# Length-1 LSTM of the first superchunk as one set of seven products, layer 2 weight products in their own tile, four pieces at other places

## The chip, the core and the metric

The kernel runs on one core of one Trainium2 chip. The metric is the device time of that core in microseconds (us). The kernel before takes 1908.22 us, the median of three runs (1907.53 to 1908.26). The profiled execution has a span of 1905.4 us, and places in the trace are given as us from its start.

TensorE is called PE in the profile (PEld its weight loads), VectorE DVE, ScalarE ACT, GpSimd POOL and SyncE SP. "L1110" is line 1110 of the kernel.

## The reference

The input x is [128 batches, 64 steps, 256 channels] in float32, with a 64 x 64 adjacency matrix. Four layers each add a residual, x = x + layer(relu(layernorm(x))):

```python
# layer 0: two products with batch normalizations, after one aggregation by the normalized adjacency
# layer 1: two graph convolutions, then LSTMs over windows of p = 1, 2, 3, 4 steps
h = relu(einsum('ts,bsh->bth', adj, x @ Wg0 + bg0))
h = relu(einsum('ts,bsh->bth', adj, h @ Wg1 + bg1))
for p in range(1, 5):
    nw = T // p
    wins = h[:, :nw * p, :].reshape(B * nw, p, H)          # windows without overlap
    last = lstm_last(Wih[p - 1], Whh[p - 1], bih[p - 1], bhh[p - 1], wins)   # zero initial state
    h = h.at[:, arange(nw) * p + (p - 1), :].set(last)     # the last step of each window
# layer 2: causal attention over the 64 steps, with Wqkv and Wo
# layer 3: attention with 4 heads, masked by the adjacency, with W
```

With p = 1 the initial state is zero, so a window is one step: three gates (input, candidate, output) from one product with Wih, then h = sigmoid(o) * tanh(sigmoid(i) * tanh(g)).

## The kernel before

The 8192 tokens are in 16 chunks of 512 tokens (8 batches by 64 steps), and the middle layers take them in 8 superchunks of two chunks. First layer 0 is computed for all chunks, because its batch normalizations need statistics of everything. Then, for superchunk 0, the two graph convolutions of layer 1 are computed alone ("first_convolutions", chunks 0 and 1); after them comes the long part of the LSTMs, superchunk after superchunk; layers 2 and 3 follow.

Products of channels by channels are computed by 2 x 2 blocks with seven products in place of eight. The seven right operands are three blocks b11, b21, b22 of the hidden state and four differences t1 = b12 - b11, t3 = b22 - b12, t2 = b22 - t1, t4 = b21 - t2 (`differences`, L313 to L316). The block rows are the two halves of the channels; the columns are two halves of the tokens. The weights' sums, which the left operands need, are formed once.

**The length-1 LSTM** is `single` (L1275): seven products by three gates, each a matmul at L1307, kinds 2, 1, 5, 6, 3, 7, 4 in that order. ScalarE copies products from PSUM (L1327), VectorE adds others to them (L1331), ScalarE applies sigmoid and tanh (L1312, L1320), GpSimd or VectorE multiplies the gates (L1317), and VectorE writes the new state into hT (L1323). The differences are all formed on GpSimd. In superchunks 1 to 7 the token halves are the first and the last 32 steps of all 16 batches, 512 columns each. In superchunk 0 there are two sets, one for each chunk, with halves of 256 columns, so that the first can begin while chunk 1's convolutions are still under way.

**The longer LSTMs** are `lstm` with p = 2, 3, 4. Each begins with a product g (L1123) for the first step, whose gates ScalarE reads from PSUM at L1110; that frees the banks in which the next products, y, z and x at L1152, are summed. Differences of the new state (hd, L313 on VectorE) precede the products with it. Gate sums are VectorE's at L1161, gate functions ScalarE's at L1066.

**The order around them is written out by hand.** `lstms` is a generator: its yields are numbered as units, 0 to 3 in the length-1 LSTM, 4 to 7 in length 2, 8 to 13 in length 3, 14 to 21 in length 4. At each unit, pieces of other work are issued: the convolutions of the next superchunks, the residual of the superchunk before, and `ahead`, which prepares layer 2. Tables say at which unit each piece comes: CONV and BEGUN (in superchunk 0 FIRST and BEGUN_FIRST) for the convolutions, RESIDUAL, AHEAD, LATE, and FINAL for the last superchunk. All engines take their instructions in that order; a piece that waits holds what was issued to its engine after it.

- A convolution's pieces are: load (normalization L898 and transposes L986 on VectorE, to DRAM and back, and the load of x), the sum L284, layer norm statistics, its application in two halves (factor nmr, L194, on VectorE, then two L196 on ScalarE for each half), aggregate, copies, product v, bound, product u, bias (L933), aggregate, and twice `to_hT` (L938, ScalarE).
- The pieces of `ahead` are: put, reorder, statistics, first half of the application (L194 and two L196), second half, and squares with put.

**Weight products.** Layer 2 uses Wq Wk^T and Wv Wo, formed once during layer 0 in `weight_products` (L717): matmuls L730, copies L732 into wqkv_sb, the tile from which Wqkv was read, and a store to DRAM at L733 (products_far, wqv_far in the profile). Two tiles ("ws", two buffers) in the same pool take the weights whose sums are formed for the LSTMs. Later the pool is closed, and the tile "early", the input of chunks 0 and 1, lies over the same memory. Pools wait by tile: a new tile waits for every user of the tiles whose memory it takes.

The lines that decide where pieces come:

```python
for n, _ in enumerate(lstms(sc, hTs[sc])):
    for u in todo.pop(n, ()):
        next(u)
```

Of the kernel before, what the change touches and what calls it, by code (L numbers as in the profile page):

```python
# [8 lines left out]
F32 = mybir.dt.float32  # L9
# [4 lines left out]
P = 128  # L14
# [5 lines left out]
def kernel(  # L20
# [22 lines left out]
    nc = tc.nc  # L43
    B, T, D = x.shape
    H0 = w1t.shape[1]
    KD = D // P
# [6 lines left out]
    CH = 512  # L53
    NJ = CH // P
    NB = CH // T
    NCH = B * T // CH
    SUP = 2
# [251 lines left out]
    def differences(engine, dst, b11, b12, b21, b22, third=None):  # L309


        t1, t2, t3, t4 = dst
        return [lambda: engine.tensor_tensor(t1, b12, b11, OP.subtract),  # L313
                lambda: ((third or engine).tensor_tensor(t3, b22, b12, OP.subtract),
                         engine.tensor_tensor(t2, b22, t1, OP.subtract)),
                lambda: engine.tensor_tensor(t4, b21, t2, OP.subtract)]  # L316
# [80 lines left out]
    class Seven1:  # L397
# [28 lines left out]
        def part(self, m, j):  # L426
            return z1whole[self.c][m][:, :, halves2[j]]
# [161 lines left out]
    with tc.manual_schedule(engines={mybir.EngineType.PE, mybir.EngineType.DVE,  # L589
# [27 lines left out]
        for c in range(2, NCH - 1):  # L617
            a, z = sevens[c], sevens.get(c - 1)
# [3 lines left out]
            b = sevens[c + 1] = Seven1(c + 1) if c + 1 < NCH - 1 else None  # L622
# [36 lines left out]
        c = NCH - 1  # L659
# [27 lines left out]
    with tc.manual_schedule(engines={mybir.EngineType.PE}):  # L687
        banks = product2([0, 1], True)
        close_l0()


        stage, close_stage = pool("stage", 1)
        wqkv_sb = stage.tile([P, KD, 3 * D], F32, name="wqkv_sb")
        wo_sb = stage.tile([P, KD, D], F32, name="wo_sb")
        bg0_sb = stage.tile([P, D], F32, name="bg0_sb")
        bg1_sb = const.tile([P, D], F32, name="bg1_sb")
        wg1_st = stage.tile([P, KD, D], F32, name="wg1_st")
        nc.sync.dma_start(wqkv_sb, wqkv.rearrange("(k p) f -> p k f", p=P))
        nc.sync.dma_start(wo_sb, wo.rearrange("(k p) f -> p k f", p=P))
        nc.sync.dma_start(bg0_sb, bg0.partition_broadcast(P))  # L700
        nc.sync.dma_start(bg1_sb, bg1.partition_broadcast(P))
        nc.sync.dma_start(wg1_st, wg1.rearrange("(k p) f -> p k f", p=P))

        wt = stage.tile([P, 3 * KD, D], F32, name="wt")
        c1 = stage.tile([P, KD, P], F32, name="c1")

        def weight_transposes(blocks):
            for f in blocks:
                ps = bank(f"wt_{f}")
                for k in range(KD):  # L710
                    nc.tensor.transpose(ps[:, k * P : (k + 1) * P],
                                        wqkv_sb[:, k, f * P : (f + 1) * P], ident)
                nc.vector.tensor_copy(wt[:, f, :], ps[:, :D])

        products = [wqkv_sb[:, :, i * D : (i + 1) * D] for i in range(2)]
        products_far = dram.tile([P, KD, 2 * D], F32, tag="wqv", name="wqv_far", bufs=1)

        def weight_products():
            for m in range(KD):
                ps = bank(f"c1_{m}")  # L720
                nc.tensor.matmul(ps[:, :P], bg0_sb[:, m * P : (m + 1) * P], adjt_bd, start=True,
                                 stop=True)
                nc.scalar.copy(c1[:, m, :], ps[:, :P])
                nc.scalar.mul(nc1[:, m, :], ps[:, :P], -1.0)
            for a in range(KD):
                for dst, lhs, rhs in ((products[0], 0, wt[:, KD : 2 * KD, :]),
                                      (products[1], 2 * KD, wo_sb)):
                    ps = bank(f"wp_{a}_{lhs}")
                    for f in range(KD):
                        nc.tensor.matmul(ps[:, :D], wt[:, lhs + f, a * P : (a + 1) * P],  # L730
                                         rhs[:, f, :], start=(f == 0), stop=(f == KD - 1))
                    nc.scalar.copy(dst[:, a, :], ps[:, :D])  # L732
            nc.scalar.dma_start(products_far, wqkv_sb[:, :, : 2 * D])  # L733
            ps = bank("c2")
            for k in range(KD):
                nc.tensor.matmul(ps[:, :D], c1[:, k, :], wg1_st[:, k, :], start=(k == 0),
                                 stop=(k == KD - 1))
            return ps

        def weight_sums(p, q):
            w = stage.tile([P, 16, P], F32, tag="ws", name=f"ws_{p}_{q}", bufs=2)
            for i, src in enumerate((wih_t, whh_t)):
                nc.sync.dma_start(
                    w[:, 8 * i : 8 * i + 4, :].rearrange("p (k c) f -> p k (c f)", k=KD),
                    src[p - 1].rearrange("(k p) f -> p k f", p=P)[:, :, q * D : (q + 1) * D])
            yield
            v = w.rearrange("p (i b) f -> p i b f", i=2)
            for dst, a, b, op in ((4, 1, 3, OP.add), (5, 4, 0, OP.subtract), (6, 0, 1, OP.subtract),  # L750
                                  (7, 2, 5, OP.subtract)):
                nc.gpsimd.tensor_tensor(v[:, :, dst], v[:, :, a], v[:, :, b], op)
            far = dram.tile([P, 15, P], F32, tag=f"ws{p}{q}", name=f"wfar_{p}_{q}", bufs=1)
            nc.sync.dma_start(far[:, :9], w[:, :9])
            nc.sync.dma_start(far[:, 9:], w[:, 10:])
            wfar[p, q] = far
            yield

        wanted = [(p, q) for p in range(2, SKIP + 1) for q in GATES]
# [3 lines left out]
    with tc.manual_schedule(engines={mybir.EngineType.PE, mybir.EngineType.DVE,  # L763
# [3 lines left out]
        for c in range(2, NCH - 1):  # L767
            a, b, z = sevens[c], sevens.get(c + 1), sevens.get(c - 1)
# [64 lines left out]
    with tc.manual_schedule(engines={mybir.EngineType.PE}):  # L833
        c = NCH - 1
# [438 lines left out]

    KINDS1 = {1: 0, 2: 1, 4: 2, 5: 3, 6: 4, 7: 5, 3: 6}

    def single(b, m, name, yields):

        wide = b[0, 0].shape[1:]  # L1280
        gates = l1.tile([P, 4, KD, CH], F32, tag="gates", name=f"gates_{name}", bufs=1)
        cells = l1.tile([P, KD, CH], F32, tag="cell", name=f"cell_{name}", bufs=1)
# [3 lines left out]
        def folded(a):  # L1286
            return a.rearrange("p (a b) -> p a b", b=wide[1]) if len(wide) > 1 else a
# [2 lines left out]
            return (more if j else cells)[:, c, :m] if g == 2 else gates[:, 2 * g + j, c, :m]  # L1290

        t = []
        for i in range(4 * m // (2 * CH)):
            part = l1.tile([P, 7 * (T // 3) * NB], F32, tag="xd", name=f"xd_{name}_{i}", bufs=2)
            t += [folded(part[:, a : a + m]) for a in range(0, 2 * CH, m)]
        for f in differences(nc.gpsimd, t, b[0, 0], b[0, 1], b[1, 0], b[1, 1]):
            f()
        right = {1: b[0, 0], 2: b[1, 0], 3: b[1, 1], 4: t[3], 5: t[0], 6: t[1], 7: t[2]}
        ys, xs_ = [[bank(f"{n}_{name}_{g}", tag) for g, tag in enumerate(tags)]
                   for n, tags in (("y1", "yyz"), ("x1", "zxx"))]  # L1300
# [4 lines left out]
        def product(kind):  # L1305
            for g in range(3):
                nc.tensor.matmul(folded(ps(g, kind)), wih1[:, g, KINDS1[kind], :], right[kind],  # L1307
                                 start=kind in (2, 5, 1), stop=True, skip_group_check=True)
# [16 lines left out]
        def copy(dst, kind):  # L1325
            for g in range(3):
                nc.scalar.copy(at(g, *dst), ps(g, kind))  # L1327

        def add(dst, kind):
            for g in range(3):  # L1330
                nc.vector.tensor_add(at(g, *dst), at(g, *dst), ps(g, kind))  # L1331

        product(2)
        copy((0, 0), 2)
        product(1)
        add((0, 0), 1)
        for g in range(3):
            act(g, 0, 0)
        cell(nc.gpsimd, 0, 0)
        if 0 in yields:  # L1340
            yield
        product(5)
        copy((1, 1), 5)
# [1 line left out]
        product(6)  # L1345
        copy((0, 1), 6)
        state(0, 0)
        if 1 in yields:
            yield
        product(3)  # L1350
        add((0, 1), 3)
        for g in range(3):
# [7 lines left out]
        act(2, 1, 1)  # L1360
        state(0, 1)
        cell(nc.vector, 1, 1)
        if 2 in yields:
            yield
        product(4)
        act(0, 1, 0, ps(0, 4))
        tanh(1, 1)
# [3 lines left out]
        tanh(1, 0)  # L1371
        state(1, 1)
        state(1, 0)
        if 3 in yields:
            yield

    def lstms(sc, hT):
        hv = hT.rearrange("p k (t b) -> p k t b", t=T)

        def views(part):  # L1380
            return {(k, j): part(hv[:, k, j * T // 2 : (j + 1) * T // 2, :]) for k in range(KD)
                    for j in range(2)}

        if sc:
            yield from single(views(lambda a: a.rearrange("p t b -> p (t b)")), CH, f"{sc}_1", range(4))
        else:
            for i in range(SUP):
                yield from single(views(lambda a: a[:, :, i * NB : (i + 1) * NB]), CH // 2, f"{sc}_1_{i}",
                                  (1, 3))
        for p in range(2, SKIP + 1):  # L1390
            yield from lstm(p, hv, f"{sc}_{p}", p == SKIP and sc < NCH // SUP - 1)

# [52 lines left out]
    RESIDUAL = (0, 3, 4), (2, 5, 6)  # L1445
    CONV = (3, 4, 4, 5, 6, 7, 8, 9, 10, 10), (3, 4, 4, 11, 12, 13, 14, 15, 16, 17, 18, 20)
    BEGUN = (11, 13, 14, 16), (17, 19)
    BEGUN_FIRST = (13, 15, 16, 18), (19, 21)
    FIRST = (0, 2, 3, 4, 4, 5, 6, 7, 8, 9, 10, 11, 12, 12), (3, 6, 7, 8, 8, 13, 14, 15, 16, 17, 18, 19, 20, 20)
    AHEAD = (4, 5, 7, 8, 14, 15), (6, 7)  # L1450
    LATE = 5, 6, 8, 9
    IDLE = {5: 4, 7: 18, 9: 10, 13: 14, 15: 8}
    FINAL = (4, 5, 10, 12, 12, 14), (6, 7, 11, 14, 14, 16)
# [595 lines left out]
```

## Time and profile before

| | us | share of the span |
|---|---|---|
| PE busy | 1869.7 | 98% |
| DVE busy | 1238.2 | 65% |
| ACT busy | 1017.2 | 53% |
| POOL busy | 578.4 | 30% |
| g of length 2 to 4, L1123 | 184.1 | |
| y, z, x of length 2 to 4, L1152, by operands: x<-xd | 285.6 | |
| span | 1905.4 | |

A page of the profile gives each engine's busy time, the granted TensorE clock, the chain of work that ended last, and the groups of instructions with, after the bar, their busy time, the mean of one in ns, and the idle time ahead of them with what ended it ("2.1 <-DVE gates L1161 1.7": 2.1 us idle, of which 1.7 were ended by that instruction). A line of the chain of waits gives start, length and what. A line of a timeline gives start, length, engine, line, operation, tiles and count, and in brackets the idle time before it and its releaser. A line of the table by windows gives the stretch, its length, busy time and count of PE, PEld, DVE, ACT and POOL, the granted clock (1.00 is full), the busy share of the DMA engines, and GB/s.

Matmuls of 512 columns follow each other every 0.86 us, those of 256 columns every 0.43 us. PE is busy nearly everywhere, so what matters are the places where it is not, and which instruction ends each wait there.

### The profile page before, as it was taken

The numbers are of one execution on the slowest core, as the hardware profiler recorded it, in microseconds if no ns is written. First come the engines' busy times: TensorE is split into PE (matmuls) and PEld (weight loads), VectorE is DVE, ScalarE is ACT, GpSimd is POOL, SyncE is SP. The second block draws the span as 40 slices with busy tenths as digits, with TensorE's granted clock in tenths as the row PEclk, the third lists the DMA queues.
The fourth block names the chain that finished last, engine by engine and source line by source line (L and its number), as shares of the span: only waits on it lengthen the run. The fifth ranks groups of instructions, "written<-read, shape, count | busy, mean of one in ns | idle before, by whom it ended". The sixth has DMA issues, their size and how long they took to land.

```text
span 1905.4 us, 39237 instructions
## 1 busy us (share of the span) xinstructions
PE 1869.7 (98%) x15119; PEld 1489.5 (78%) x15119; DVE 1238.2 (65%) x3157; ACT 1017.2 (53%) x2309; POOL 578.4 (30%) x766
## 2 busy tenths in 40 slices
PE   8999989999999999999999999999999999999998
PEld 6877866886897789689689679868959967777776
DVE  6768745567566666667657666665565567776776
ACT  5766535446456455555645644655565544444453
POOL 5856622123222222322322232222122113332332
PEclk9999989999999999999999999999999999999999
DMA  3223642134333533333433443333144245454433
GB/s 113 79 67 148 223 175 93 58 117 172 117 128 128 160 128 112 104 119 138 150 116 129 149 138 133 133 111 109 52 146 141 101 139 150 136 154 143 135 112 112
DMA packets 111403, 241.48 MB, mean 127 GB/s; under 512 B 11504, under 2 KB 74864, under 8 KB 111216
## 3 DMA queue, kind: packets, MB, share of 16 engines
q1 hardware_dynamic: 110192, 237.09, 37.0%
q8 instruction: 120, 1.97, 0.4%
q0 software_dynamic: 320, 1.05, 0.2%
q10 hardware_dynamic: 704, 0.82, 0.1%
q14 instruction: 67, 0.55, 0.1%
HBM read 170.50 MB, written 68.42 MB: 125 GB/s over the span
## 4 chain that ended last, share of the span: by engine, by line
PE 82%; DVE 8%; ACT 4%; POOL 2%; issue 2%; DMA 1%; SPq 0%; DVEq 0%; ACTq 0%
PE x L1152 22%; PE z L1152 11%; PE g L1123 7%; PE y L1152 5%; PE v L1539 5%; PE x L1307 3%; PE p_q L1546 3%; PE y L1307 3%; PE X L1735 3%; PE v L913 3%; PE X L423 2%; PE X L499 2%; PE u L927 2%; PE Y L1735 1%; PE Y L423 1%
## 5 line engine op out<-in xcount | busy, mean ns | idle before, releaser
L1161 DVE TENSOR_TENSOR gates<-gates,x 128x128 f32<-128x128 f32 (+2 forms) x384 | 118.3, 320 | 314.2 <-PE x L1152 312.0
L1152 PE MATMUL x<-xd,wset 128*128 128x128 f32 (+2 forms) x1280 | 285.6, 311 | 2.1 <-DVE gates L1161 1.7
L1152 PE MATMUL x<-hd,wset 128*128 128x128 f32 (+2 forms) x1152 | 246.7, 303 | 0.0
L1210 POOL TENSOR_TENSOR gates<-gates 128x512 f32<-128x512 f32 (+2 forms) x48 | 74.9, 1560 | 521.8 <-ACT gates L1066 521.8
L1152 PEld LDWEIGHTS x<-xd,wset 128*128 128x128 f32 x1280 | 202.1, 190 | 20.1 <-DVE gates L1161 6.1
L1066 ACT ACTIVATE gates<-gates,bias 128x256 f32<-128x256 f32 (+4 forms) x384 | 170.4, 490 | 65.0 <-DVE gates L1161 61.6
L1152 PEld LDWEIGHTS x<-hd,wset 128*128 128x128 f32 x1152 | 185.1, 191 | 5.0
L1123 PE MATMUL g<-hT,wset 128*128 128x256 f32 (+2 forms) x576 | 184.1, 474 | 1.9 <-DVE hT L1077 1.1
L1123 PEld LDWEIGHTS g<-hT,wset 128*128 128x128 f32 x576 | 108.4, 190 | 70.8 <-issue 38.0
L1158 ACT COPY gates<-y 128x128 f32<-128x128 f32 (+2 forms) x192 | 54.2, 293 | 194.4 <-PE y L1152 193.8
L1152 PE MATMUL z<-hs,wset 128*128 128x128 f32 (+2 forms) x768 | 154.0, 303 | 0.0
L1152 PEld LDWEIGHTS z<-hs,wset 128*128 128x128 f32 x768 | 119.8, 191 | 3.3
L1158 ACT COPY gates<-x 128x128 f32<-128x128 f32 (+2 forms) x192 | 56.5, 295 | 93.8 <-PE x L1152 92.9
L1161 DVE TENSOR_TENSOR gates<-gates,z 128x128 f32<-128x128 f32 (+2 forms) x384 | 104.5, 315 | 0.1
L1066 ACT ACTIVATE gates<-x,bias 128x128 f32<-128x128 f32 (+2 forms) x192 | 74.7, 389 | 49.1 <-PE x L1152 46.2
L1152 PE MATMUL z<-hT,wset 128*128 128x128 f32 (+1 forms) x512 | 97.1, 302 | 0.0
L1152 PE MATMUL x<-hs,wset 128*128 128x128 f32 (+2 forms) x384 | 84.9, 303 | 0.0
L1152 PE MATMUL y<-xd,wset 128*128 128x128 f32 (+2 forms) x384 | 78.2, 306 | 3.9 <-ACT gates L1110 3.9
L1152 PE MATMUL y<-hd,wset 128*128 128x128 f32 (+2 forms) x384 | 80.1, 311 | 1.9 <-DVE hd L313 1.9
L1221 ACT ACTIVATE gates<-cell 128x256 f32<-128x256 f32 (+2 forms) x144 | 55.3, 384 | 49.9 <-DVE cell L1220 49.8
L1110 ACT ACTIVATE gates<-g,bias 128x512 f32<-128x512 f32 (+2 forms) x144 | 72.3, 557 | 17.7 <-PE g L1123 17.6
L1554 POOL TENSOR_TENSOR s<-s,mx 128x256 f32<-128x256 f32 (+2 forms) x33 | 40.4, 1225 | 129.6 <-DVE mx L1553 121.8
(328 smaller groups left out, 4278.9 us busy)
## 6 DMA issues: line engine op xcount, KB each, us to landing
wset<-wfar SPq DMA_DIRECT2D x96, 960.0 KB, 6.6
hT<-far_h SPq DMA_DIRECT2D x124, 128.0 KB, 3.1
far_h<-hm SPq DMA_DIRECT2D x16, 512.0 KB, 3.0
far_n<-xs SPq DMA_DIRECT2D x16, 512.0 KB, 3.7
xs<-far_n SPq DMA_DIRECT2D x64, 128.0 KB, 3.8
far_x<-xs SPq DMA_DIRECT2D x16, 512.0 KB, 3.0
x<-far_x SPq DMA_DIRECT2D x64, 128.0 KB, 3.3
xt<-in_x_dram SPq DMA_DIRECT2D x15, 512.0 KB, 4.0
```

The lines of the kernel that those rows point to most:

```text
L423: nc.tensor.matmul(self.banks[tag][:, i * CH // 2 : (i + 1) * CH // 2], w, self.at[kind], start=first and not i, stop=True, skip_group_che ...
L913: nc.tensor.matmul(banks[m], wg0_sb[:, k, m * P : (m + 1) * P], agg[:, k, :], start=(k == 0), stop=(k == KD - 1))
L1066: nc.scalar.activation(gate(q, c, part), src, AF.Tanh if q == 2 else AF.Sigmoid, bias=bs[:, q * KD + c : q * KD + c + 1])
L1110: nc.scalar.activation(columns_of(gate(q, c)), natural(banks[q, c][:, :n].rearrange("p (w b) -> p w b", b=nb)), AF.Tanh if q == 2 else AF. ...
L1123: nc.tensor.matmul(banks[q, c][:, :n].rearrange("p (w b) -> p w b", b=nb), wsets[p, q][:, 2 * k + c, :], hv[:, k, : (nw - 1) * p + 1 : p, ...
L1152: nc.tensor.matmul(folded(self.psum(kind)), wsets[p, self.q][:, BLOCKS[kind][i], :], (ox[self.s] if part == "x" else oh)[kind], start=firs ...
L1158: nc.scalar.copy(gate(self.q, kind // 5, halves[kind // 5]), self.psum(kind))
L1161: nc.vector.tensor_add(gate(self.q, *dst), gate(self.q, *a), self.psum(kind))
L1210: nc.gpsimd.tensor_mul(gates[:, 0, :, :n], gates[:, 0, :, :n], gates[:, 2, :, :n])
L1307: nc.tensor.matmul(folded(ps(g, kind)), wih1[:, g, KINDS1[kind], :], right[kind], start=kind in (2, 5, 1), stop=True, skip_group_check=True)
L1539: nc.tensor.matmul(ps[:, i, :], hT[:, k, j, :], w[:, k, first : first + D], start=(k == 0), stop=(k == KD - 1))
L1735: nc.tensor.matmul(st[c, tag][:, i * CH // 2 : (i + 1) * CH // 2].rearrange("p (a n) -> p a n", n=P), w, st[c, "o7"][kind], start=first an ...
```

## The change

It has four parts.

- The layer 2 weight products go to a tile of their own, ws_p, a third use of the tag "ws"; so wqkv_sb is only read, and the store no longer stands between it and "early".
- `single` is always one set of 512 columns a half. In superchunk 0 the halves of the tokens are the two chunks, so that product 2, which needs chunk 0 alone, can be issued first; a yield after it issues the last aggregate of chunk 1's convolution, and the differences follow. In the other superchunks the differences come first, as before.
- The first difference, t1, is formed on VectorE, in all eight superchunks; the other three stay with GpSimd.
- Places: BEGUN_FIRST's first piece from 13 to 12 (load of conv 4 in superchunk 0), FIRST's first three to 1, 3, 3 (the units of `single` in superchunk 0 mean other places now), FIRST's second half of the application of conv 3 from 8 to 10, and AHEAD's fourth, the first half of the application of the layer norm for layer 2, from 8 to 12 (superchunks 1 to 6).

```diff
-        products = [wqkv_sb[:, :, i * D : (i + 1) * D] for i in range(2)]
         def weight_products():
+            products_sb = stage.tile([P, 16, P], F32, tag="ws", name="ws_p", bufs=2)[:, : 4 * KD]
+            products_sb = products_sb.rearrange("p (k c) f -> p k (c f)", k=KD)
+            products = [products_sb[:, :, i * D : (i + 1) * D] for i in range(2)]
...
-            nc.scalar.dma_start(products_far, wqkv_sb[:, :, : 2 * D])
+            nc.scalar.dma_start(products_far, products_sb)
...
-        for f in differences(nc.gpsimd, t, b[0, 0], b[0, 1], b[1, 0], b[1, 1]):
-            f()
...
+        first = differences(nc.vector, t, b[0, 0], b[0, 1], b[1, 0], b[1, 1])[:1]
+        rest = differences(nc.gpsimd, t, b[0, 0], b[0, 1], b[1, 0], b[1, 1])[1:]
+        if begun:
+            for f in first + rest:
+                f()
         product(2)
         copy((0, 0), 2)
+        if not begun:
+            yield
+            for f in first + rest:
+                f()
         product(1)
...
-        if 0 in yields:
+        if begun:
             yield
         product(5)
...
-        if sc:
-            yield from single(views(lambda a: a.rearrange("p t b -> p (t b)")), CH, f"{sc}_1", range(4))
-        else:
-            for i in range(SUP):
-                yield from single(views(lambda a: a[:, :, i * NB : (i + 1) * NB]), CH // 2, f"{sc}_1_{i}",
-                                  (1, 3))
+        def tokens(k, j):
+            if sc:
+                return hv[:, k, j * T // 2 : (j + 1) * T // 2, :].rearrange("p t b -> p (t b)")
+            return hv[:, k, :, j * NB : (j + 1) * NB]
+
+        yield from single({(k, j): tokens(k, j) for k in range(KD) for j in range(2)}, f"{sc}_1", sc > 0)
...
-    BEGUN_FIRST = (13, 15, 16, 18), (19, 21)
-    FIRST = (0, 2, 3, 4, 4, 5, 6, 7, 8, 9, 10, 11, 12, 12), (3, 6, 7, 8, 8, 13, 14, 15, 16, 17, 18, 19, 20, 20)
-    AHEAD = (4, 5, 7, 8, 14, 15), (6, 7)
+    BEGUN_FIRST = (12, 15, 16, 18), (19, 21)
+    FIRST = (1, 3, 3, 4, 4, 5, 6, 7, 8, 9, 10, 11, 12, 12), (3, 6, 7, 8, 10, 13, 14, 15, 16, 17, 18, 19, 20, 20)
+    AHEAD = (4, 5, 7, 12, 14, 15), (6, 7)
```

More of the change, by code (lines that the diff above doesn't have):

```diff
@@ L1274, with single @@
     KINDS1 = {1: 0, 2: 1, 4: 2, 5: 3, 6: 4, 7: 5, 3: 6}
-    def single(b, m, name, yields):
+    def single(b, name, begun):
+        m = CH
         wide = b[0, 0].shape[1:]
@@ L1292, in single @@
         t = []
-        for i in range(4 * m // (2 * CH)):
+        for i in range(2):
             part = l1.tile([P, 7 * (T // 3) * NB], F32, tag="xd", name=f"xd_{name}_{i}", bufs=2)
-            t += [folded(part[:, a : a + m]) for a in range(0, 2 * CH, m)]
-        for f in differences(nc.gpsimd, t, b[0, 0], b[0, 1], b[1, 0], b[1, 1]):
-            f()
+            t += [folded(part[:, a : a + m]) for a in range(0, 2 * m, m)]
         right = {1: b[0, 0], 2: b[1, 0], 3: b[1, 1], 4: t[3], 5: t[0], 6: t[1], 7: t[2]}
@@ L1347, in single @@
         state(0, 0)
-        if 1 in yields:
-            yield
+        yield
         product(3)
@@ L1362, in single @@
         cell(nc.vector, 1, 1)
-        if 2 in yields:
-            yield
+        yield
         product(4)
@@ L1373, in single @@
         state(1, 0)
-        if 3 in yields:
-            yield
+        yield
     def lstms(sc, hT):
         hv = hT.rearrange("p k (t b) -> p k t b", t=T)
-        def views(part):
-            return {(k, j): part(hv[:, k, j * T // 2 : (j + 1) * T // 2, :]) for k in range(KD)
-                    for j in range(2)}
-        if sc:
-            yield from single(views(lambda a: a.rearrange("p t b -> p (t b)")), CH, f"{sc}_1", range(4))
-        else:
-            for i in range(SUP):
-                yield from single(views(lambda a: a[:, :, i * NB : (i + 1) * NB]), CH // 2, f"{sc}_1_{i}",
-                                  (1, 3))
+        def tokens(k, j):
[3 more added lines that the diff above has]
+        yield from single({(k, j): tokens(k, j) for k in range(KD) for j in range(2)}, f"{sc}_1", sc > 0)
         for p in range(2, SKIP + 1):
```

## The prediction

> **What bounds the kernel now.** I read the page first, then the chain of waits, then the timelines of single engines around each edit.
>
> ```profile
> PE 1869.7 (98%) x15119; PEld 1489.5 (78%) x15119; DVE 1238.2 (65%) x3157; ACT 1017.2 (53%) x2309; POOL 578.4 (30%) x766
> PE 82%; DVE 8%; ACT 4%; POOL 2%; issue 2%; DMA 1%; SPq 0%; DVEq 0%; ACTq 0%
> L1152 PE MATMUL y<-xd,wset 128*128 128x128 f32 (+2 forms) x384 | 78.2, 306 | 3.9 <-ACT gates L1110 3.9
> L1152 PE MATMUL y<-hd,wset 128*128 128x128 f32 (+2 forms) x384 | 80.1, 311 | 1.9 <-DVE hd L313 1.9
> ```
>
> TensorE is busy 1869.7 of 1905.4 us, so only some 36 us of idle, plus matmuls stretched by late operands, can be won. The change takes no matmul work away: 42 products of 256 columns at 0.43 us and 21 of 512 at 0.86 us are both 18.1 us. It is worth only the stalls it closes. The two last lines show stalls of 3.9 and 1.9 us that recur with the superchunks. The chain of waits between 220 and 345 us shows the one large hole:
>
> ```profile
> 240.27 3.47 PE wp L730 x16
> 244.16 3.12 DMA wqv_far<-wqkv_sb
> 247.36 3.96 DMA early<-in_x_dram
> 257.11 1.20 PE agg_b L214 x30
> ```
>
> The weight products' store must land before the input tile "early", which lies over the same memory, may load. The timelines of ScalarE, VectorE and TensorE confirm what waits:
>
> ```profile
> 247.38 2.22 ACT L895 ACTIVATE cv<-z1a,sh_bn,sc_bn 128x512 f32<-128x512 f32 x3 [3.25 <-DMA wqv_far<-wqkv_sb]
> 251.44 0.69 DVE L956 TENSOR_TENSOR xs<-early,at_b 128x512 f32<-128x512 f32 x1 [3.49 <-DMA early<-in_x_dram]
> 248.25 3.68 PE L239 MATMUL at_b<-ident,cv 128*128 128x128 f32 x16 [3.67 <-ACT cv L895]
> 245.00:255.00 10.00, 6.38 (x32) 6.14 (x32) 3.90 (x11) 2.22 (x3) 0.95 (x2) 0.66 0.79 240
> ```
>
> The last line (busy time by windows) has the granted clock, 0.66, after that idle; the next ten microseconds have 0.83. The timelines at the other edits: the first length-3 LSTM of superchunk 1 (AHEAD), that of superchunk 0 (FIRST), then conv 4 (BEGUN_FIRST).
>
> ```profile
> 510.47 1.09 ACT L196 ACTIVATE h<-xs,nmr_n,rstd_n 128x256 f32<-128x256 f32 x2 [4.59 <-DVE nmr_n L194]
> 511.46 1.81 ACT L1110 ACTIVATE gates<-g,bias 128x336 f32<-128x336 f32 x4
> 512.13 0.89 PE L1152 MATMUL y<-xd,wset 128*128 128x168 f32 x4 [0.30 <-ACT gates L1110]
> 347.32 2.07 ACT L196 ACTIVATE cv<-xs,nmr_b,rstd_b 128x256 f32<-128x256 f32 x4 [4.59 <-DVE nmr_b L194]
> 403.84 1.29 DVE L284 TENSOR_TENSOR xs<-xs,cv 128x512 f32<-128x512 f32 x2 [5.52 <-DMA xs<-in_x_dram]
> 405.39 0.49 PE L1152 MATMUL x<-xd,wset 128*128 128x128 f32 x2 [1.71 <-DVE gates L1161]
> ```
>
> In each, normalization or residual work stands in an engine's queue ahead of the gate work that frees TensorE's next bank.
>
> **What the Trainium skill says.** "Perfetto Trace Analysis", section Tensor Engine Instruction: ScalarE, VectorE and GpSimd queues are strictly in order. The trace agrees: L1110 starts at 511.46, when L196 ends, although its first bank was complete by 509. "TensorE: Matmul & The Clock Gate", Part 1: an idle window of some 3.4 us halves the clock. The trace agrees: 0.66 after 3.67 us idle. "SBUF — State Buffer", two separate sides: a VectorE operation with two SBUF inputs and a GpSimd operation exclude each other. The trace agrees: L1317 on VectorE took 0.95 us at 290.45, beside GpSimd's L314, and 0.42 at 302.09 alone.
>
> **The change part by part.**
>
> *Products in their own tile.* Before, "early" waits for copies L732 and store L733. After, it waits only for the transposes that read wqkv_sb (end 232.1) and an issue of SyncE up to 233.9; at 4 us it lands near 240, before it is needed. L895 then follows the store's issue (244.16 + 0.61) instead of its landing: 244.8, not 247.38, 2.6 us earlier. The transposes L239 move to 245.7, and L956 needs their end only: its two banks allow about 246.4, not 251.44, 5.0 earlier. With idle cut to about 1 us the clock stays higher: the 16 idle_d fillers (2.91 us here, 1.75 at the 0.109 each of the transposes L711 at 231.22, eight in 0.87) lie in slack, v and aggregate perhaps bring 0.4. One load of the length-1 weights now waits for the store (247.3), but GpSimd reads them at 257: hidden. Sum −5.4 us; bounds −4.5 (some DVE or GpSimd step of the chain binds) and −6.0.
>
> *One set of seven in superchunk 0.* Before, TensorE's stalls here are 0.74 + 0.22 + 1.42 + 0.69 + 0.25 = 3.3 us (timeline: 0.58 on L1331, 1.26 on L1327, 0.53 on L1331 as idle, the rest stretched matmuls), and g L1123 starts at 302.22. Laid out again: product 2 at 279.07 (it waits for L933 as before), the aggregate of conv 1 to 282.7, product 1 to 285.3, product 5 at 285.5 once VectorE's L313 ends, products 6, 3, 7 and 4 at 2.58 each: g at 298.5, 3.7 earlier. But conv 2's pieces come later: its load (L898, L986) ends at 293.5, not 287.5, and its states land near 302.4. On VectorE there follow L284 (1.3), statistics (2.2), conv 3's load (2.3) and L194, to 308.5; then L196 x4 (2.08 us) hold ScalarE to 310.6, and only then comes L1110, which frees the banks. Before, L1110 began at 311.58 and y L1152 at 312.60. So y starts near 311.5: of the 3.7 us only 1.1 stay, and TensorE waits 2.2 us for ScalarE. Sum −1.1; bounds −3.3 and +0.5.
>
> *First difference on VectorE.* A difference of 512 columns takes 0.69 us on VectorE, 1.27 on GpSimd (1.72 at 447.49, overlapped). Product 5 waits for it only in superchunk 1 (0.26 idle, 0.42 with the stretch: −0.4). In superchunk 7 GpSimd's chain ends 1.27 earlier, so that the wait of g at 1403.74 (0.70 on L1323, 0.87 with stretch) mostly goes: −0.8. In superchunks 2 to 6 TensorE has no gap there and VectorE has idle before the adds: 0. Sum −1.2; bounds 0 and −1.4.
>
> *FIRST, 8 to 10.* Two of the four L196 at 347.32 leave; L1110 moves from 349.30 to 348.3, and the stall at 349.97 (1.30 us, nearly all of it) closes: −1.0 (0.5 to 1.1). The other two fit idle ScalarE time at unit 10.
>
> *BEGUN_FIRST, 13 to 12.* Conv 4's load runs at 391.50 on VectorE; one unit earlier it falls into the 4.96 us idle before 384.66, where its 2.3 us are hidden. Its data land about 12 us sooner, at 394 to 396, before L284's turn at 398.3. The 5.52 us VectorE wait goes, and with it TensorE's stall at 405.39: −1.75 (0.8 to 1.87). FIRST's opening (0, 2 to 1, 3) only follows the new yields.
>
> *AHEAD, 8 to 12.* In superchunks 1 to 6, at 512, 669, 826, 983, 1139 and 1296 us, L194 and two L196 (1.09 us) stand ahead of L1110. TensorE loses 0.30 on y<-xd and 0.32 on y<-hd as idle (six times 0.32 is the page's 1.9; six times 0.30 and the 1.3 at 349.97 are most of its 3.9), and as much again in matmuls stretched to ScalarE's pace: start-to-start times exceed their usual value by 1.29 in all. Without the half, L1110 keeps TensorE's pace. At unit 12 ScalarE is idle 2.29 us (from 701.61) and VectorE 3.76, room for 1.09 and 0.35. Sum 6 x −1.29 = −7.7; bounds: six times the idle plus a little, −4.0, and −8.2.
>
> Total −5.4 − 1.1 − 1.2 − 1.0 − 1.75 − 7.7 = −18.2: 1908.2 − 18.2 = 1890.
>
> **The rivals.** *More from the single set:* conv 2's transfers land sooner than I placed them, L196 ends before 309, and nearly all 3.3 us stay with the clock's 0.4 in part A: −20.8, 1887. For it: far loads here take 3 to 4 us; against: five steps in series. *Half of AHEAD:* the half at unit 12 goes in ahead of L1066, or the stretched matmuls have another cause (the pace of L1110 itself), and only the pure idle of 0.62 goes: −4.0 in place of −7.7, 1894; with part B at +0.5 and C at 0, 1897. For it: ScalarE paces y and z after a short g anyway. Against: length-3 g in superchunk 0 shows the same stall with L196 ahead. *Wait for wait, slower:* the moved half delays L1066 by its 1.08 in all six superchunks (+6.5), the wide single leaves TensorE waiting for VectorE, whose queue now has L313 and conv 2 ahead of the gate adds (+3.3), and the other parts give nothing, since each closed hole is waited out at the next step: 1918. Against: unit 12's idle time is longer than the work.
>
> **How the numbers follow.** Forecast 0.55 (1890), more 0.17 (1887), half 0.24 (1894 to 1897), slower 0.04 (1918). The range reaches over the first three with the bounds of A and B: 1885 to 1898.5. Of the third case 0.02 could end within 0.2% (3.8 us) of 1908.2, so faster 0.94, same 0.02, slower 0.04.
>
> **What would show it.** Part A: the transposes L239 start near 245.7, after an idle of about 1 us, and L956 no longer names the DMA. Part B: g starts about 3.7 us earlier relative to product 2, with an idle of y<-xd on L1110 of about 2 us. AHEAD: the waits of y on L1110 and on hd L313 fall from 3.9 and 1.9 to below 3 and near 0, with no new TensorE wait on L1161 in the last length-3 units. BEGUN_FIRST: the 1.71 us at 405.39 is gone. I am wrong if a gate addition L1161 or L1066 shows new waits, or if products 5 or 6 wait for GpSimd in the wide single.

## The result, and the profile after

The kernel after takes 1899.53 us (median of four runs, 1899.39 to 1901.76), against 1908.24 us before in the same comparison: a ratio of 0.9957, with a 95% interval of 0.9940 to 0.9974. That is 8.7 us less, where 18.2 were forecast, and just outside the range (1885 to 1898.5). The direction was right, and half of the gain is missing.

First the page after: busy time of the engines, the chain's shares, and the two groups of matmuls that were shown of before.

```profile
PE 1862.9 (98%) x15077; PEld 1478.2 (78%) x15077; DVE 1238.9 (65%) x3150; ACT 1015.9 (54%) x2284; POOL 569.7 (30%) x752
PE 86%; DVE 7%; POOL 3%; ACT 2%; issue 1%; DMA 0%; DVEq 0%; SPq 0%; ACTq 0%
L1154 PE MATMUL y<-xd,wset 128*128 128x128 f32 (+2 forms) x384 | 77.4, 304 | 3.4 <-ACT gates L1112 3.4
L1154 PE MATMUL y<-hd,wset 128*128 128x128 f32 (+2 forms) x384 | 80.1, 311 | 0.0
```

(Lines lie 1 to 3 later than before: L1152 is L1154, L1110 is L1112.) The wait of y on hd, 1.9 us, is gone as forecast. POOL has risen from 2 to 3% of the chain. The table of TensorE's waits (total, times, longest) says why, in a line that the kernel before does not have:

```profile
PE z L1154 <- POOL xd L1097: 9.5, 6, 1.7
PE y L1154 <- ACT gates L1112: 3.4, 3, 2.3
```

A new wait for GpSimd, 9.5 us in six pieces, one for each superchunk in which AHEAD's piece was moved.

**Where the time went.** The two traces hold the same matmuls in nearly the same order, so each matmul can be paired with its counterpart. The difference of the two start times, drawn over the execution, is a curve that moves only where time is won or lost. Its steps, with what the prediction gave each part:

| part | forecast, us | step in the trace, us |
|---|---|---|
| products in their own tile | −5.4 | −5.3 |
| one set in superchunk 0 | −1.1 | −0.7 (−3.3 up to g, +2.6 at y and z) |
| FIRST 8 to 10 | −1.0 | −1.0 |
| BEGUN_FIRST 13 to 12 | −1.75 | −2.0 |
| first difference on VectorE, superchunk 1 | −0.4 | +0.6 |
| the same, superchunk 7 | −0.8 | −1.0 |
| AHEAD 8 to 12, six superchunks | −7.7 | +3.4 |
| elsewhere: superchunk 6 (+0.75), layers 2 and 3 (−1.3), the last store (−1.5) | 0 | −2.05 |
| sum | −18.2 | −8.05 (the span: 1905.4 to 1897.3, −8.1) |

Four parts came within 0.4 us of what was worked out. AHEAD is 11.1 us off, more than the whole difference. The entries of "elsewhere" lie at none of the places that the change edits, and they differ from one kernel to the next: with two sets in superchunk 0, or conv 3's load one unit later (both below), superchunk 6 lacks 0.6 or 0.3 us of its +0.75, and the −1.3 are for the most part waits of layer 3's score matmuls for "issue". They are not claimed for the change, so some 2 us of the gain are no credit to the prediction.

**The hole behind the store**, in the timelines of ScalarE, VectorE and TensorE, and busy time by windows:

```profile
244.54 2.22 ACT L897 ACTIVATE cv<-z1a,sh_bn,sc_bn 128x512 f32<-128x512 f32 x3 [0.49 <-PE c L738]
246.16 0.69 DVE L958 TENSOR_TENSOR xs<-early,at_b 128x512 f32<-128x512 f32 x1 [1.07 <-PE at_b L239]
245.41 1.20 PE L239 MATMUL at_b<-ident,cv 128*128 128x128 f32 x9 [0.91 <-ACT cv L897]
245.00:255.00 10.00, 7.51 (x104) 5.88 (x105) 7.48 (x23) 4.53 (x8) 2.83 (x6) 1.00 0.88 313
```

No line names the DMA any more, TensorE's idle is 0.91 in place of 3.67, and the granted clock is 1.00 in place of 0.66. What L897 waits for now is the last product on TensorE ahead of it (L738), not the issue of the store.

**AHEAD**, at the same place as before's lines at 510 to 512 (the first length-3 LSTM of superchunk 1), in the timelines of ScalarE, GpSimd, VectorE and TensorE:

```profile
500.63 2.23 ACT L1112 ACTIVATE gates<-g,bias 128x336 f32<-128x336 f32 x4 [3.17 <-PE g L1125]
500.14 0.23 POOL L99 TENSOR_SCALAR rstd_n<-mv_n 128x4 f32<-128x4 f32 x1 [12.65 <-DVE mv_n L160]
500.45 1.04 POOL L100 TENSOR_TENSOR rstd_n<-rstd_n,mhalf 128x4 f32<-128x4 f32 x1
503.96 1.51 POOL L1097 COPY xd<-hT 128x168 f32<-128x168 f32 x3
502.33 1.29 DVE L1118 TENSOR_TENSOR cell<-gates 128x336 f32<-128x336 f32 x2 [1.11 <-ACT gates L1112]
503.83 0.54 DVE L1077 TENSOR_TENSOR hs<-gates 128x336 f32<-128x336 f32 x1 [0.22 <-ACT gates L1112]
503.25 0.73 PE L1154 MATMUL y<-xd,wset 128*128 128x168 f32 x4
505.53 1.41 PE L1154 MATMUL z<-xd,wset 128*128 128x168 f32 x8 [1.54 <-POOL xd L1097]
```

The first line and the y line are the forecast: L1112 now follows g's own pace, and y starts without a wait. But z needs operands that GpSimd copies (L1097; length 3 has an odd number of windows, so the blocks are copied), and the reciprocal root of layer 2's preparation (L99, L100) stands ahead of them in GpSimd's queue. GpSimd waits 12.65 us for its statistics; during the last 3.5 of these the states from which the copies are made were ready (VectorE wrote the last at 497.91). GpSimd, VectorE and TensorE in the kernel before:

```profile
508.56 0.23 POOL L99 TENSOR_SCALAR rstd_n<-mv_n 128x4 f32<-128x4 f32 x1 [12.65 <-DVE mv_n L160]
511.96 0.86 POOL L1095 COPY xd<-hT 128x168 f32<-128x168 f32 x3
512.87 1.57 DVE L1116 TENSOR_TENSOR cell<-gates 128x336 f32<-128x336 f32 x2 [2.44 <-ACT gates L1110]
512.99 1.46 PE L1152 MATMUL z<-xd,wset 128*128 128x168 f32 x8
```

There the copies ended at 512.82 and z began at 512.99: a second limit stood 0.17 us behind ScalarE's and showed no wait. Counted from the start of g (504.89 before, 496.47 after), the copies ended after 7.93 us before and after 9.00 now. In the kernel before, VectorE was idle for 2.44 us, until 512.87, while GpSimd formed these operands; now its gate work, which follows L1112, runs beside them: L1118 beside the last differences, L1077 beside the copies. So z starts 0.96 us later from g than before; the end of y's wait on hd, with its stretch, gives 0.39 back, which leaves the step of this superchunk, about +0.57.

**BEGUN_FIRST and the single set**, TensorE's and VectorE's timelines after:

```profile
390.30 1.29 DVE L284 TENSOR_TENSOR xs<-xs,cv 128x512 f32<-128x512 f32 x2
293.54 10.46 PE L1125 MATMUL g<-hT,wset 128*128 128x512 f32 x24
306.32 1.18 PE L1154 MATMUL y<-xd,wset 128*128 128x256 f32 x4 [2.31 <-ACT gates L1112]
```

L284 no longer waits for a DMA (5.52 us before), and the 1.71 us of x on L1161 are gone. In superchunk 0, g starts 8.7 us earlier than before and y only 6.3: that is the wait of 2.31 us on L1112, forecast as 2.2.

### The profile page after: what moved, and what is told of

Read it like the earlier page. It is cut to its first block, busy times and chain, and to the rows that moved or that the text cites. A ratio compares the mean times of both kernels' runs of the same rounds, so it can differ in the third digit from the quotient of the medians.

```text
span 1897.3 us, 39092 instructions
## 1 busy us (share of the span) xinstructions
PE 1862.9 (98%) x15077; PEld 1478.2 (78%) x15077; DVE 1238.9 (65%) x3150; ACT 1015.9 (54%) x2284; POOL 569.7 (30%) x752
## 4 chain that ended last, share of the span: by engine, by line
PE 86%; DVE 7%; POOL 3%; ACT 2%; issue 1%; DMA 0%; DVEq 0%; SPq 0%; ACTq 0%
PE x L1154 22%; PE z L1154 11%; PE g L1125 7%; PE v L1542 6%; PE y L1154 5%; PE x L1308 4%; PE y L1308 3%; PE p_q L1549 3%; PE v L915 3%; PE X L1738 3%; PE X L423 2%; PE X L499 2%; PE u L929 2%; PE Y L1738 1%; PE Y L423 1%
## 5 line engine op out<-in xcount | busy, mean ns | idle before, releaser
L1154 PE MATMUL x<-xd,wset 128*128 128x128 f32 (+2 forms) x1280 | 285.6, 311 | 0.7 <-DVE gates L1163 0.2
L1154 PE MATMUL x<-hd,wset 128*128 128x128 f32 (+2 forms) x1152 | 246.7, 303 | 0.0
L1154 PEld LDWEIGHTS x<-xd,wset 128*128 128x128 f32 x1280 | 202.1, 190 | 19.1 <-DVE gates L1163 6.1
L1154 PEld LDWEIGHTS x<-hd,wset 128*128 128x128 f32 x1152 | 185.1, 191 | 5.0
L1154 PE MATMUL z<-hs,wset 128*128 128x128 f32 (+2 forms) x768 | 154.0, 303 | 0.0
L1154 PEld LDWEIGHTS z<-hs,wset 128*128 128x128 f32 x768 | 119.8, 191 | 3.3
L1154 PE MATMUL z<-hT,wset 128*128 128x128 f32 (+1 forms) x512 | 97.1, 302 | 0.0
L1112 ACT ACTIVATE gates<-g,bias 128x512 f32<-128x512 f32 (+2 forms) x144 | 74.5, 559 | 32.1 <-PE g L1125 31.6
L1154 PE MATMUL x<-hs,wset 128*128 128x128 f32 (+2 forms) x384 | 84.8, 303 | 0.0
L1154 PE MATMUL y<-xd,wset 128*128 128x128 f32 (+2 forms) x384 | 77.4, 304 | 3.4 <-ACT gates L1112 3.4
L1154 PE MATMUL y<-hd,wset 128*128 128x128 f32 (+2 forms) x384 | 80.1, 311 | 0.0
L1154 PEld LDWEIGHTS z<-hT,wset 128*128 128x128 f32 x512 | 76.7, 191 | 3.9 <-ACT gates L1112 0.6
```

The lines of the kernel that those rows point to most:

```text
L1112: nc.scalar.activation(columns_of(gate(q, c)), natural(banks[q, c][:, :n].rearrange("p (w b) -> p w b", b=nb)), AF.Tanh if q == 2 else AF. ...
L1154: nc.tensor.matmul(folded(self.psum(kind)), wsets[p, self.q][:, BLOCKS[kind][i], :], (ox[self.s] if part == "x" else oh)[kind], start=firs ...
```

## The experiments

The theory after the traces is called **GpSimd**: AHEAD's move did free the gate work L1112, but z then waits for GpSimd, whose queue holds the reciprocal root ahead of the length-3 operands. The main rivals are **ScalarE**, by which the prediction's step holds and another part costs the time, and **unit 12**, by which the moved half costs at its new place. Medians are given with the ratio to the kernel before on the same chip.

### AHEAD alone, and everything but AHEAD

On the kernel before, one edit:

```diff
-    AHEAD = (4, 5, 7, 8, 14, 15), (6, 7)
+    AHEAD = (4, 5, 7, 12, 14, 15), (6, 7)
```

> Kernel before with one edit: AHEAD's fourth entry 8 to 12. Theory GpSimd (the gate work L1110 is freed, but z of the length-3 LSTM then waits for the copies L1095, which stand in GpSimd's queue behind the reciprocal root L99/L100 of the same preparation, and which run slower beside VectorE's earlier cell products): the loss of 0.53 us that the two traces show at each of the six superchunks is the edit's own, so 1908.2 + 3.2 = 1911.4 us, and the trace has six waits of z on xd L1095 of about 1.5 us. Rival ScalarE (the prediction's step was right, and another part of the change costs the time): 1908.2 - 7.7 = 1900.5 us.

Measured: 1913.57 us (before 1908.88), ratio 1.0024 (1.0014 to 1.0034), so slower by 4.7 us. The steps in the trace at the six superchunks sum to +3.7, and TensorE's waits begin with:

```profile
PE z L1152 <- POOL xd L1095: 9.6, 6, 1.8
```

The loss is the edit's own, and the step of the prediction had the wrong sign. Now the reverse, on the kernel after:

```diff
-    AHEAD = (4, 5, 7, 12, 14, 15), (6, 7)
+    AHEAD = (4, 5, 7, 8, 14, 15), (6, 7)
```

> Kernel after with AHEAD's fourth entry back at 8. Theory GpSimd: 1899.5 - 3.2 = 1896.3 us, with the waits of y on L1112 and on hd L313 of the kernel before (0.30 and 0.32, six times) back. Rival ScalarE: 1899.5 + 7.7 = 1907.2 us.

Measured: 1898.94 us, ratio 0.9945 (0.9933 to 0.9958). The rival ScalarE, with 1907.2, is excluded. The steps at the six superchunks sum to −3.4, and the waits of y on hd L313 (2.0 us, six times) are back. The median is only 0.6 us below the kernel after's in its own comparison, though the ratios differ by 2.3 us; the profiled execution lost 1.4 us near 308 us, where the clock was cut (last section).

### Statistics one unit later

On the kernel after: GpSimd forms the length-3 operands before it comes to the reciprocal root, since the statistics' piece is issued in the length-3 LSTM's first unit and not before it.

```diff
-    AHEAD = (4, 5, 7, 12, 14, 15), (6, 7)
+    AHEAD = (4, 5, 8, 12, 14, 15), (6, 7)
```

> Kernel after with the statistics of the same preparation one unit later (AHEAD's third entry 7 to 8), so that GpSimd forms the length-3 operands before it waits for VectorE's statistics; the first half of the application stays at 12. Theory GpSimd: operands can begin when the last state of length 2 is written, some 3.5 us sooner, and the copies end before y is issued; the loss of 0.53 and the forecast gain of 1.29 per superchunk both come: 6 x 1.82 = 10.9, 1888.6 us, with the copies L1097 back at 0.86 us for three. Rival unit 12 (the half application at unit 12 is what costs): no change, 1899.5 us. Rival pace (only the pure idle was ScalarE's): 6 x (0.53 + 0.62) = 6.9, 1892.6 us.

Measured: 1889.52 us, ratio 0.9900 (0.9886 to 0.9913). The six steps against the kernel after are −1.74 to −1.97, in sum −11.0. GpSimd and TensorE at the same place:

```profile
500.53 0.86 POOL L1097 COPY xd<-hT 128x168 f32<-128x168 f32 x3
502.29 0.23 POOL L99 TENSOR_SCALAR rstd_n<-mv_n 128x4 f32<-128x4 f32 x1 [0.89 <-DVE mv_n L160]
504.55 1.30 PE L1154 MATMUL z<-xd,wset 128*128 128x168 f32 x8
```

The copies come before L99, take 0.86 us again, and z follows y without a wait. Both rivals of this run fall: the half at unit 12 costs nothing that shows, and the stretched matmuls were due to ScalarE too. Against the kernel before, the six steps sum to 3.4 − 11.0 = −7.6; the forecast for AHEAD was −7.7. The release was sized rightly. What it released into was not looked at.

### Copies on ScalarE

On the kernel after, the statistics stay at unit 7:

```diff
-                    nc.gpsimd.tensor_copy(t[4 + i], b[kj])
+                    if s == 1:
+                        nc.scalar.copy(t[4 + i], b[kj])
+                    else:
+                        nc.gpsimd.tensor_copy(t[4 + i], b[kj])
```

> Kernel after with the three operand copies L1097 of the first step of length 3 on ScalarE in place of GpSimd, where ScalarE is idle 3.2 us ahead of L1112; statistics stay at unit 7. Theory GpSimd: z no longer waits for GpSimd's queue; as much as with the later statistics if the copies fit the idle time, 1888.6 us, and up to 6 x 0.5 more if L1112 starts later by part of them, 1891.6 us. Rival unit 12: 1899.5 us.

Measured: 1889.52 us, ratio 0.9895 (0.9882 to 0.9909); steps −1.81 to −1.97, in sum −11.2. A second way to take the same wait away, without touching the order of the statistics, gives the same gain by the steps. So it is the copies' end on GpSimd that held z.

### The tile alone

On the kernel before, only the weight products' own tile (the first and second hunk of the change).

> Kernel before with the products' own tile alone. Theory (the hole behind the store is closed and nothing later gives it back): the step of -5.3 us that the two traces show near 254 us, so 1908.5 - 5.3 = 1903.2 us, with the idle of at_b on L895 at about 1.1 us. Rival (a part of the step came from other edits, or a later wait takes it back, since only L895 moves by 2.6 us): 1908.5 - 2.6 = 1905.9 us.

Measured: 1904.22 us (before 1909.42), ratio 0.9972 (0.9962 to 0.9981): −5.2 us. The step in the trace is −5.3, and TensorE's wait for the load's scaling (L897) 0.90 us. The theory holds. The profiled execution (1905.5 us) gave 1.8 of it back near 402 us, by a cut of the clock (last section).

### Two sets, and the difference on GpSimd

First the kernel after with the two sets of before in superchunk 0 (256 columns a half), and only the first difference on VectorE. The edit is shown against the kernel before, and the other parts of the change are in it too:

```diff
+        for f in differences(nc.vector, *args)[:1] + differences(nc.gpsimd, *args)[1:]:
+            f()
...
+    FIRST = (0, 2, 3, 4, 4, 5, 6, 7, 8, 9, 10, 11, 12, 12), (3, 6, 7, 8, 10, 13, 14, 15, 16, 17, 18, 19, 20, 20)
```

> Kernel after with two sets of seven products in superchunk 0 (one for each chunk, as before; FIRST begins at 0, 2, 3 again), everything else as in after. Theory (the one set gains 3.3 us to g, and 2.6 of them go back in the wait of y on L1112): 1899.5 + 0.8 = 1900.3 us. Rival (what y waits for there has another cause, so that the two sets would have it too): 1899.5 + 3.3 = 1902.8 us.

Measured: 1902.97 us, ratio 0.9966 (0.9953 to 0.9978). The steps in superchunk 0 are +2.6 up to g and −2.7 at y and z: the waits there cancel, as the theory has it, and y has no wait of 2.3 us, against the rival. But the time is 2.8 us above the kernel after's on the same chip (1900.18, the run with conv 3's load later), not 0.8. The trace has those microseconds in layers 2 and 3, partly as waits for "issue" (steps of +0.9, −0.6, +0.8 and +1.2), and I have no cause for them. So by the steps the one set alone is worth nothing here, and the −0.7 of the table is what the first difference on VectorE gains in superchunk 0 (next run). By the measured times the one set's worth is open between 0 and 3 us.

Then the kernel after with all four differences on GpSimd:

```diff
-        first = differences(nc.vector, t, b[0, 0], b[0, 1], b[1, 0], b[1, 1])[:1]
+        first = differences(nc.gpsimd, t, b[0, 0], b[0, 1], b[1, 0], b[1, 1])[:1]
```

> Kernel after with the first difference of the length-1 LSTM on GpSimd again, in all superchunks. Theory (on VectorE it stands behind the residual sum L284 in superchunk 1 and runs beside GpSimd's L314, which costs 0.6 us, and gains 1.0 us in superchunk 7): steps of -0.6 at superchunk 1 and +1.0 at 7, in sum +0.4, 1899.9 us. Rival (the prediction's: gains in both): steps of +0.4 and +0.8, 1900.7 us. The time hardly tells them apart; the steps of the trace do.

Measured: 1903.87 us, ratio 0.9971 (0.9960 to 0.9982). That is 3.7 us above the next run, which has the time of the kernel after on the same chip; 0.4 was expected. The steps are −0.6 in superchunk 1 and +1.0 in 7, as the theory has them, and a third, +0.7, in superchunk 0, which I had missed: product 5 starts 0.4 us later there, since it follows the differences closely, and product 4 another 0.3. Of the rest, +0.6 at 258 us and +1.2 at 308 go with granted clocks of 0.78 and 0.84 (255 to 260 and 305 to 310 us), where the kernel after has 1.00.

### Conv 3's load later

On the kernel after, to take the 2.31 us of y away:

```diff
-    FIRST = (1, 3, 3, 4, 4, 5, 6, 7, 8, 9, 10, 11, 12, 12), (3, 6, 7, 8, 10, 13, 14, 15, 16, 17, 18, 19, 20, 20)
+    FIRST = (1, 3, 3, 4, 4, 5, 6, 7, 8, 9, 10, 11, 12, 12), (4, 6, 7, 8, 10, 13, 14, 15, 16, 17, 18, 19, 20, 20)
```

> Kernel after with the load of conv 3 (L900 and the transposes, 2.3 us on VectorE) one unit later, FIRST's second row from 3 to 4, so that it comes after the factor L194 of conv 2's normalization. Theory (y in superchunk 0 waits 2.3 us for ScalarE because L194 stands behind that load on VectorE): L194 and L196 come 2.3 us earlier, y hardly waits, 1899.5 - 2.2 = 1897.3 us. Rival (ScalarE gets to L1112 late for conv 2's transfers themselves, or the load now delays the cell products after L1112 as much): 1899.5 us.

Measured: 1900.18 us, ratio 0.9952 (0.9940 to 0.9965), no change, so the expectation was a miss. Its timelines of VectorE and TensorE:

```profile
302.75 0.69 DVE L194 SCALAR_TENSOR_TENSOR nmr_b<-mv_b,rstd_b 128x4 f32<-128x4 f32 x1 [1.48 <-POOL rstd_b L100]
303.37 1.90 DVE L900 TENSOR_SCALAR cv<-z1a,sc_bn,sh_bn 128x512 f32<-128x512 f32 x2
306.27 1.18 PE L1154 MATMUL y<-xd,wset 128*128 128x256 f32 x4 [2.08 <-ACT gates L1112]
```

The load does come after L194, but L194 now waits for GpSimd's reciprocal root instead and ends where it did before: the load had been standing in a wait of nearly the same length. The prediction's chain had counted the load (2.3 us) and left out the root, which lies between statistics and L194; it came out right by luck, because one hides the other.

### The kernel after again, two places alone, and two further versions

For these four, on one chip: the kernel after unchanged,

> The kernel after once more, on the chip of the next three, as their measure. Nothing is changed: 1899.5 us, and the six waits of z on xd L1097 again.

measured 1901.54 us (before 1908.78), ratio 0.9956 (0.9943 to 0.9968), and the six waits of z on xd L1097 are there again (9.5 us). The kernel before with superchunk 0's two places:

```diff
-    BEGUN_FIRST = (13, 15, 16, 18), (19, 21)
+    BEGUN_FIRST = (12, 15, 16, 18), (19, 21)
...
-    FIRST = (0, 2, 3, 4, 4, 5, 6, 7, 8, 9, 10, 11, 12, 12), (3, 6, 7, 8, 8, 13, 14, 15, 16, 17, 18, 19, 20, 20)
+    FIRST = (0, 2, 3, 4, 4, 5, 6, 7, 8, 9, 10, 11, 12, 12), (3, 6, 7, 8, 10, 13, 14, 15, 16, 17, 18, 19, 20, 20)
```

> Kernel before with the two places of superchunk 0 alone: BEGUN_FIRST's first 13 to 12, FIRST's second row 8 to 10. Theory (each closes its stall and nothing takes it back, as the steps of the two traces have it): -1.0 and -1.9, so 1908.8 - 2.9 = 1905.9 us, with x no longer waiting for L1161 near 405 us. Rival (the stall comes back at the next wait): 1908.8 us.

Measured: 1905.52 us, ratio 0.9981 (0.9973 to 0.9989), −3.3 us; the steps are −1.0 and −2.0, and no wait of x on L1161 is left. Both steps of the prediction hold. On the kernel after, the statistics at unit 8, and in superchunk 1 the first difference on GpSimd:

```diff
+        first = differences(nc.gpsimd if name == "1_1" else nc.vector, t, b[0, 0], b[0, 1], b[1, 0], b[1, 1])[:1]
...
+    AHEAD = (4, 5, 8, 12, 14, 15), (6, 7)
```

> Kernel after with the statistics of AHEAD at unit 8, and the first difference on GpSimd in superchunk 1 alone. Theory (in superchunk 1 the difference on VectorE stands behind the sum L284): 1889.5 - 0.6 = 1888.9 us, and no wait of product 5 on xd L313 on VectorE. Rival (product 5 waits for GpSimd as long, as in before): 1889.3 us or more. The step in the trace tells, the time hardly.

Measured: 1887.83 us, ratio 0.9888 (0.9875 to 0.9902), the step at superchunk 1 against the version before it −0.75. This beats both kernels: 21 us below before, 13.7 below after, on the same chip. Product 5 still waits 0.25 for GpSimd there, in place of 0.88 for VectorE. Last, with conv 2's application moved behind L1112:

```diff
+        if split:
+            yield
         for j in range(NJ):
...
+    FIRST = (1, 3, 3, 4, 5, 5, 6, 6, 7, 8, 9, 10, 11, 12, 12), (3, 6, 7, 8, 10, 13, 14, 15, 16, 17, 18, 19, 20, 20)
```

> As best_a, and in superchunk 0 the factor L194 of conv 2's normalization stays at unit 4, its four L196 go to unit 5, aggregate and copies to 6, so that ScalarE comes to L1112 of length 2 before them. Theory (y waits 2.3 us there because the L196 stand ahead of L1112): 1888.9 - 2.3 = 1886.6 us. Rival (the L196 then hold up the copies of y, L1160, behind them as much): 1888.9 us.

Measured: 1887.95 us, ratio 0.9886 (0.9873 to 0.9900), no change against the version before it. TensorE and VectorE:

```profile
304.65 1.03 PE L1156 MATMUL y<-xd,wset 128*128 128x256 f32 x4
327.02 1.28 DVE L286 TENSOR_TENSOR xs<-xs,cv 128x512 f32<-128x512 f32 x2
328.69 0.70 PE L1156 MATMUL x<-xd,wset 128*128 128x256 f32 x2 [1.00 <-DVE gates L1165]
```

y no longer waits, but most of the gain is gone by 328 us: 0.60 us as a wait for hd, the aggregate's 1.1 us only moved behind, and 1.00 us because the aggregate's copies and the sum L286 now stand on VectorE ahead of the gate sums L1165. The 0.7 us that remain by the steps are lost again in layers 2 and 3, most of them to a longer wait for "issue". The rival's end is right, by another wait than it named.

## Why the prediction was right or wrong

- **Tile: right.** −5.4 forecast, −5.3 in the trace, −5.2 alone. The banks and the clock came as worked out; the issue, put at 0.6 us, took 0.35, and L897 started 0.3 us earlier than forecast, when L738 was done.
- **One set: the sum is right, the credit is not.** g came 3.3 us earlier (3.7 forecast), then y waited 2.31 (2.2 forecast; the prediction's own 3.7 − 1.1 gives 2.6, which is the whole step at y and z). But the plan had the first difference on VectorE in it, and without that the one set gains nothing by the steps. The term inside the wait was named wrongly: conv 3's load is not on the path alone; GpSimd's root would hold L194 as long.
- **First difference: half right.** Superchunk 7 gained 1.0 (0.8 forecast). Superchunk 1 lost 0.6, where 0.4 was to be won: there the sum L284 stands ahead on VectorE (437.50 to 439.06), and the difference then took 1.75 us beside GpSimd's L314, not 0.69. The prediction took the price of the difference alone, though it had quoted that the two engines exclude each other. Superchunk 0's 0.7 us were in the plan of the one set ("once VectorE's L313 ends") and not priced apart.
- **FIRST and BEGUN_FIRST: right,** −1.0 and −2.0 in the trace, −3.3 for both without the rest (−2.75 forecast).
- **AHEAD: the step that failed.** It read "Without the half, L1110 keeps TensorE's pace." It does, but that was taken for the last wait. z needs GpSimd's copies, which ended 0.17 us before z began, so at this place z could not start more than 0.17 us earlier, and the gate work that VectorE now does earlier made the copies end 1.07 us later. Measured +3.4 (+3.7 alone) in place of −7.7. With the operands ahead of the root in GpSimd's queue the full 7.6 us come. The rivals looked for the trouble at unit 12, where there is none, and none of the prediction's signs of being wrong looked at z's operands.
- **The range** ended at 1898.5 because its upper case kept half of AHEAD; no case had AHEAD lose while the rest held, which is what happened.

## What to carry to other kernels

Before a wait is priced at its full length, look up when every other operand of the instruction behind it is ready: a second input that lands just before the instruction starts shows no wait in any table, and caps the gain. Follow its engine's queue back to what stands at its head; here an instruction waited 12.65 us for statistics, for the last 3.5 with unrelated work ready behind it, and moving it by one unit was worth 11.0 us, about as much as the rest of the change together. And an engine that is freed runs beside others at new times: look which instructions then take longer.

## What the runs showed of the hardware that was not expected

**The clock after short waits.** An idle of 1.9 to 2.3 us on TensorE is in some executions followed by a cut clock, with the same program. In superchunk 0, after y's wait on L1112, the kernel after's two profiled executions read, in busy time by windows (first the execution shown above, then the repeated one):

```profile
301.24:304.65 3.41, 2.77 (x7) 0.95 (x5) 2.22 (x5) 1.12 (x3) 3.33 (x5) 1.00 0.18 72
304.65:308.07 3.42, 1.75 (x7) 1.02 (x8) 0.72 (x2) 3.24 (x6) 0.94 (x2) 1.00 0.47 167
```

```profile
304.02:307.44 3.42, 1.17 (x5) 0.48 (x4) 0.00 (x0) 3.42 (x7) 2.03 (x3) 1.00 0.38 155
307.44:310.85 3.41, 3.41 (x10) 2.66 (x10) 2.33 (x4) 3.22 (x6) 0.00 (x0) 0.50 0.93 211
```

The clock stayed at 1.00 in the one and fell to 0.50 for 3.41 us in the other, which lost 1.35 us there after a wait of 2.25 us. The windows are chosen from the traces: in each of the fourteen, the granted clock changes only at whole multiples of 3.41 us from its first rise, which comes 6 to 9 us into the execution. So the time falls into slots of 3.41 us. In the repeated execution the whole wait lies in one slot; in the first it is spread over two, with 0.64 us idle in the one and 1.67 in the other. Between the first rise and the last 10 us, every slot in which TensorE was idle for 1.88 us or more, eight in all, was followed by a slot at 0.50. Of the slots at full clock with 1.83 us of idle or less, only seven were, all between 249 and 259 us, with 1.4 to 1.6 us of idle; why those is open. So whether a wait of some 2 us is followed by a cut clock goes with where it falls in these slots, and that differs between executions of one program. No run moved a wait on purpose to test it.

The hole behind the store fits: in the kernel before the clock fell at 246.92 us, when TensorE had been idle for 2.34 us, and not after the whole 3.67, as the prediction reads it:

```profile
244.58:246.92 2.34, 0.01 (x1) 0.00 (x0) 0.00 (x0) 0.00 (x0) 0.00 (x0) 1.00 0.59 224
246.92:248.25 1.33, 0.00 (x0) 0.00 (x0) 0.55 (x1) 0.86 (x2) 0.00 (x0) 0.50 0.00 0
```

The tile alone had 0.50 for 3.41 us after x's wait of 1.88 us, and lost 1.8. So a wait of this length can cost nearly twice its length, which may also explain some of the spread between runs (1902.86 to 1906.78 for the tile alone).

**VectorE beside GpSimd.** Three copies of 168 columns on GpSimd took 0.86 us beside an idle VectorE (the kernel before) and 1.51 beside L1077 and L313, which have two inputs in SBUF, the on-chip memory (the kernel after); a difference of 512 columns on VectorE took 0.69 alone and 1.75 beside L314 on GpSimd. This agrees with the exclusion that the Trainium skill states ("SBUF — State Buffer", SBUF: two separate sides); the sizes are these traces'. L900 has only one input and took longer beside GpSimd as well: 1.90 for two beside GpSimd's differences in the run with conv 3's load later, 0.97 for the same two in the kernel after.
